# An AdaLN transformer block: row scores copied out of their PSUM banks before the softmax

## The chip, the cores and the metric

The kernel runs on one core of a Trainium2 chip. The time is the device time of one execution in microseconds (us). The profile is one execution taken by the hardware profiler. The engines in it are PE (TensorE matmuls), PEld (TensorE weight loads), DVE (VectorE), ACT (ScalarE), POOL (GpSimd) and SP (SyncE, which issues nearly all DMA here). Each engine works through its own queue in order; an instruction that waits holds up all that stand behind it on that engine.

## The reference

`x` is (8, 1024, 512), viewed as eight sequences; a modulation vector from `cond` gives shift, scale and gate. The block is

```python
mod = silu(condition) @ Wada + bada          # six parts
xm  = layernorm(x) * (1 + sc_a) + sh_a
q, k, v = split(xm @ Wqkv)                   # 16 heads of 32
attn = softmax(where(causal, q k^T * scale, -inf))
x = x + gt_a * ((attn @ v) @ Wproj + bproj)
xm = layernorm(x) * (1 + sc_m) + sh_m
x = x + gt_m * (gelu(xm @ W1 + b1) @ W2 + b2)
```

All of it is float32.

## The kernel before

**Tiling.** The 8 x 1024 tokens are cut into 16 blocks `n` of 512 tokens, two for each sequence. Heads are taken in four groups `g` of four heads. The large products (q, k, v, up, down) are done by a Strassen scheme, so each of them is seven smaller products whose results are combined by ACT and DVE as they leave the three single PSUM banks `bank`. All products of this kind are issued from one helper (line 217) and are called the linear work below.

**Two kinds of attention.** Odd blocks, and the first two, compute the scores twice: once for the row maxima (`sc`, line 1613) and once transposed (`st`, line 1721), with the exponential on ACT (line 1734). The second half of a sequence attends to 1,024 keys, so it is always done that way. The even blocks from n = 2 on (seven of them: 2, 4, ... 14) are done "by rows", in `attend_rows` and `rows_unit` (line 1998). Their stretch of the time is called a row stage. A row stage has ten units. A unit is one query tile of 128 rows against 512 keys, or two query tiles whose widths add to 512 (384 + 128, or 256 + 256), for four heads.

**One row unit.** PE writes its scores `rows_sc` into four PSUM banks at once (line 2021). These four banks are one tile with the tag `st` and one buffer; the score units and the transposed scores of the other blocks use the same tile. DVE adds the causal mask in place (line 2028), takes the row maximum of each query tile (line 2032) and turns it into a bias (line 2034). ACT makes the exponentials from PSUM into an SBUF page `rows_p`, one instruction for each head and query tile, each followed by the reading of its sum (line 2040). When the last exponential is done, PE may write the next scores. After that DVE transposes the page in 32 x 32 blocks (line 2053), SP sends it to an image in DRAM (line 2068, `scatter`), and when an image of a head group is whole, SP fetches it back as `turned` pages (line 2143) and PE multiplies them with v (line 2155). There are three pages (`p0` to `p2`), shared by the raw pages of row units (at most two between issue and scatter, counted in `raws`) and by the fetched pages.

**What sets the order.** The program is written out once by a planner in the kernel's own Python: it keeps a planned clock for each engine (`now`), adds a planned duration for each instruction (`note`, `note_act`, `note_dma`), and remembers when a tile is planned to be written (`written`) or free (`left`). Linear work is a set of generators; before a score or row unit, `step_aside` (line 1471) goes on with linear work while the unit would have to wait longer for its tile than the linear work. `until` (line 1467) does linear work until a condition holds. DVE work that can be put off stands in `row_jobs` and `jobs` and is issued by `run_row_jobs` (line 560) and `run_jobs` when DVE is planned to be at most 2 us ahead of PE; row jobs come first. So planned durations decide the order of all instructions on all queues, that of the DMA issues on SP too; on the chip the order is fixed and semaphores make each instruction wait for its data.

The weights for the linear work go through a ring of eight SBUF buffers filled by SP (lines 358 to 362).

Of the kernel before, what the change touches and what calls it, by code (L numbers as in the profile page):

```python
# [22 lines left out]
def kernel(  # L23
# [44 lines left out]
    HPG = P // hd  # L68
# [13 lines left out]
    small = ctx.enter_context(tc.tile_pool(name="small", bufs=2))  # L82
# [12 lines left out]
    written, left = {}, {}  # L95
# [17 lines left out]
    def note(engine, ns, reads=(), writes=(), port=False):  # L113
        start = max(now[engine], due(reads, writes))
        if port:
            start = max([start] + [b for a, b in pool_spans if a <= start < b])
        end = start + ns
        now[engine] = end
        if engine == "POOL":
            pool_spans.append((start, end))  # L120
            del pool_spans[:-16]
        for k in reads:
            left[k] = max(left.get(k, 0.0), end + SYNC)
        for k in writes:
            written[k] = end + SYNC
        return end
# [19 lines left out]
    def note_act(ns, func, reads=(), writes=()):  # L146
        if func is not None and table[0] != func:
            table[0] = func
            ns += TABLE
        note("ACT", ns, reads, writes)  # L150
# [1267 lines left out]
    def start(it):  # L1418
        thread = [it, None]
        sides.append(thread)  # L1420
        advance(thread)
# [127 lines left out]
    def diagonals(parts, sc):  # L1549

        if parts[-1][4] == parts[0][4]:
            first, span = parts[0][3] - P, len(parts) * P
            return span, sc[:, :, first : first + span].rearrange("p j (a c) -> p j a c", c=P)
        return 2 * P, sc.rearrange("p j (a c) -> p j a c", c=2 * P)[:, :, :, P:]
# [443 lines left out]
    def rows_unit(n, g, parts):  # L1998

        until(lambda: n in projected)  # L2000
        until(lambda: free_p and len(raws) < 2)
        slot = take_slot()
        raws.append(slot)
        reads = [("qT", n), ("kT", n)]
        step_aside(reads, ["st", ("p", slot)])
        name = f"{n}_{g}_{parts[0][0]}"
        sc = ps_st.tile([P, HPG, TB], F32, tag="st", name=f"rows_sc_{name}")
        raw = pp.tile([P, HPG * TB], F32, tag=f"p{slot}", name=f"rows_p_{name}")
        mx, minus = (
            small.tile([P, 2, HPG], F32, tag=f"rows_{kind}", name=f"rows_{kind}_{name}")  # L2010
            for kind in ("max", "minus")
        )
        for gg in {part[4]: None for part in parts}:
            if (n, gg) not in totals_of:
                totals_of[n, gg] = small.tile(
                    [P, HPG, NTT], F32, tag=f"rows_sum_{gg}", name=f"rows_sum_{n}_{gg}", bufs=1
                )
        for qt, kh, c0, w, gg in parts:
            for j in range(HPG):
                r = slice(j * hd, (j + 1) * hd)  # L2020
                nc.tensor.matmul(  # L2021
                    sc[:, j, c0 : c0 + w], qTs[n][r, gg, ts(qt, P)], kTs[n][r, gg, :w],
                    start=True, stop=True, skip_group_check=True,
                )
            note_pe(2 * COLUMN * w, "rows", reads, ["st"])
        span, place = diagonals(parts, sc)
        shape_of = mask.unsqueeze(1).unsqueeze(1)
        nc.vector.tensor_tensor(place, place, shape_of.to_broadcast(place.shape), ALU.add)
        note("DVE", 165 + 4.16 * span, ["st"])
        n_parts = len(parts)  # L2030
        for i, (qt, kh, c0, w, gg) in enumerate(parts):
            nc.vector.tensor_reduce(mx[:, i, :], sc[:, :, c0 : c0 + w], axis=AX.X, op=ALU.max)
            note("DVE", 170 + 4.14 * w, ["st"], [("mxr", slot)])
        nc.vector.tensor_scalar(minus[:, :n_parts], mx[:, :n_parts], -scale, None, ALU.mult)  # L2034
        note("DVE", 120, [], [("mxr", slot)], port=True)
        places, at = [], 0
        for i, (qt, kh, c0, w, gg) in enumerate(parts):
            tile_of = raw[:, at : at + HPG * w].rearrange("p (b k j x) -> p j k b x", b=NTT, j=HPG, x=hd)
            for j in range(HPG):
                nc.scalar.activation(  # L2040
                    tile_of[:, j], sc[:, j, c0 : c0 + w].rearrange("p (k b x) -> p k b x", b=NTT, x=hd),
                    AF.Exp, bias=minus[:, i, j : j + 1], scale=scale, accum_out=totals_of[n, gg][:, j, qt : qt + 1],
                )
                note_act(480 + 0.82 * w, "exp", ["st", ("mxr", slot)], [("p", slot)])
            places.append((qt, w, gg, at))
            at += HPG * w
            in_sums[n, gg] += 1
            if in_sums[n, gg] == NTT:
                written["sums", n, gg] = written["p", slot]
                start(inverses(n, gg))  # L2050

        def turned():
            nc.vector.transpose(raw, raw)  # L2053
            note("DVE", 2320, [("p", slot)], [("p", slot)])
            start(scatter())

        def scatter():
            yield [("p", slot)], []
            for qt, w, gg, at in places:
                count = w // P  # L2060
                if (n, gg) not in images:
                    images[n, gg] = [
                        kept.tile([P, 2, NTT, size, P], F32, tag=f"image_{gg}_{size}", name=f"image_{n}_{gg}_{size}")
                        for size in (2, 4)
                    ]
                for a in range(NTT):
                    into = images[n, gg][qt // 2][:, qt % 2, a, :count, :]
                    nc.sync.dma_start(
                        into.rearrange("(b k) s e -> k b (s e)", k=hd),
                        raw[ts(a, hd), at : at + HPG * w].rearrange("k (b f) -> k b f", b=NTT),  # L2070
                    )
                    note_dma(230 * count, [("p", slot)])
                in_image[n, gg] += count
            left["p", slot] = now["DMA"] + LAND
            raws.remove(slot)
            give_slot(slot)
            for gg in {part[4]: None for part in parts}:
                if in_image[n, gg] == 10:
                    written["image", n, gg] = now["DMA"] + LAND + LATE / 2
                    start(gather(n, gg))  # L2080

        row_jobs.append((turned, [("p", slot)]))

    def inverses(n, g):

# [202 lines left out]
```

## Time and profile before

| | |
|---|---|
| median of 3 runs | 3538.62 us (3537.95 to 3542.44) |
| the profiled execution | 3545.22 us |
| its span | 3543.5 us |
| PE busy | 3377.7 us (95%) |
| DVE busy | 2339.5 us (66%) |
| ACT busy | 1248.8 us (35%) |
| POOL busy | 1762.9 us (50%) |
| mean granted TensorE clock | 0.985 |

A row of a group reads: line, engine, operation, output <- inputs, shapes, count | busy time in us, mean ns of one | idle time of the engine just before them and what ended it. A row of waits reads: who waited <- for whom: total us, times, longest us. A row of the timeline reads: start, length in us, engine, line, operation; in square brackets the idle time before it and what ended it. A row of a stretch reads: from:to, its length, busy time (and count) of PE, PEld, DVE, ACT and POOL, then the mean granted clock, the share of time in which the DMA engines were busy, and GB/s.

### The profile page before, as it was taken

What the parts mean: (1) busy time and instruction counts of PE and PEld (TensorE: products, weight loads), DVE (VectorE), ACT (ScalarE), POOL (GpSimd) and SP (SyncE); (2) the same over time, 40 slices, a digit from 0 to 9 for tenths busy, and PEclk for the clock granted to TensorE, in tenths of its full rate; (3) what the DMA queues carried; (4) which work ended last, traced back from release to release, by engine and by line L of the source; (5) the groups of instructions that cost most, each with busy time, mean ns of one, the idle gap of its engine ahead of it and who ended that gap; (6) DMA issues with size and microseconds to landing.
All of it is one profiled execution on the core that took longest, in us unless ns stands there. A gap on an engine that the chain in (4) does not pass through costs nothing.

```text
span 3543.5 us, 118795 instructions
## 1 busy us (share of the span) xinstructions
PE 3377.7 (95%) x52861; PEld 1705.4 (48%) x52861; DVE 2339.5 (66%) x2562; ACT 1248.8 (35%) x1970; POOL 1762.9 (50%) x1710
## 2 busy tenths in 40 slices
PE   8999889999899998999999999999999999899999
PEld 4444445444454444544454454544555445454455
DVE  5766577657577575775767757676677667566563
ACT  2334333343233532335223353333523334232521
POOL 3667713756037650477405674066731667208640
PEclk9999999999999999999999999999999999999999
DMA  6843487537875378753886538865498555973344
GB/s 198 263 148 112 150 235 214 155 109 213 245 209 155 102 226 239 209 153 103 247 233 189 153 109 264 253 185 142 127 284 236 147 142 154 284 221 111 92 135 138
DMA packets 502579, 645.42 MB, mean 182 GB/s; under 512 B 40365, under 2 KB 334061, under 8 KB 498485
## 3 DMA queue, kind: packets, MB, share of 16 engines
q1 hardware_dynamic: 501952, 637.80, 60.8%
q8 instruction: 416, 6.82, 0.8%
q14 instruction: 95, 0.77, 0.1%
q10 hardware_dynamic: 116, 0.03, 0.0%
HBM read 506.31 MB, written 129.27 MB: 179 GB/s over the span
## 4 chain that ended last, share of the span: by engine, by line
PE 37%; DMA 6%; POOL 4%; DVE 3%; issue 1%; SPq 1%; ACT 1%; DVEq 0%; POOLq 0%; ACTq 0%
PE bank L217 27%; PE sc L1613 3%; POOL pT L1856 3%; PE po L1762 2%; PE st L1721 2%; DMA held_m<-xm_m 1%; DMA turned<-image 1%; PE rows_sc L2021 1%; PE st L1709 1%; PE po L2155 1%; DVE mx L1628 1%; DMA w<-in_L_cond_Wproj_dram 1%; DMA hat_m<-held_m 1%; PE bank L1783 0%; DMA w<-in_L_cond_W_dram 0%
## 5 line engine op out<-in xcount | busy, mean ns | idle before, releaser
L1856 POOL TENSOR_TENSOR pT<-pT,pT 128x512 f32<-128x512 f32 (+3 forms) x918 | 981.9, 1104 | 250.5 <-ACT pT L1734 197.2
L217 PE MATMUL bank<-w,hT 128*32 128x256 f32 x14336 | 822.4, 380 | 0.9 <-ACT y_d L204 0.9
L1734 ACT ACTIVATE pT<-st 128x2048 f32<-128x2048 f32 x218 | 409.5, 1879 | 762.1 <-PE st L1721 573.9
L217 PEld LDWEIGHTS bank<-w,hT 128*32 128x32 f32 x14336 | 457.0, 110 | 372.7 <-issue 87.5
L1628 DVE TENSOR_REDUCE mx<-sc 128x4 f32<-128x2048 f32 (+3 forms) x271 | 499.4, 1859 | 183.0 <-PE sc L1613 179.7
L217 PE MATMUL bank<-xm_m,w 128*32 128x256 f32 x8192 | 506.6, 384 | 28.8 <-DMA w<-in_L_cond_W_dram 19.7
L2040 ACT ACTIVATE rows_p<-rows_sc,rows_minus 128x256 f32<-128x256 f32 (+3 forms) x448 | 229.6, 534 | 448.0 <-DVE rows_minus L2034 246.4
L217 PE MATMUL bank<-t_m,w 128*32 128x256 f32 x6144 | 382.9, 380 | 1.1 <-DVE hT L208 0.9
L217 PEld LDWEIGHTS bank<-xm_m,w 128*32 128x32 f32 x8192 | 257.8, 111 | 245.5 <-issue 66.4
L217 PEld LDWEIGHTS bank<-t_m,w 128*32 128x32 f32 x6144 | 190.7, 110 | 179.8 <-issue 58.3
L217 PE MATMUL bank<-xm_a,w 128*32 128x256 f32 x3968 | 252.1, 392 | 26.0 <-DVE xm_a L782 16.3
L217 PE MATMUL bank<-w,qT 128*32 128x512 f32 x2048 | 242.0, 610 | 16.3 <-DMA w<-in_L_cond_Wproj_dram 16.2
L1613 PE MATMUL sc<-kT,qT 32*128 32x512 f32 (+3 forms) x2168 | 250.6, 546 | 6.9 <-DVE mx L1628 3.5
L1762 PE MATMUL po<-pT,v 128*32 128x512 f32 (+3 forms) x2176 | 232.0, 515 | 4.5 <-POOL pT L1739 4.4
L1721 PE MATMUL st<-qT,kT 32*128 32x512 f32 (+3 forms) x2176 | 228.5, 508 | 0.0
L208 DVE TENSOR_TENSOR hT<-bank,u_u 128x512 f32<-128x512 f32 x181 | 121.4, 683 | 113.0 <-PE bank L217 110.6
L217 PEld LDWEIGHTS bank<-xm_a,w 128*32 128x32 f32 x3968 | 131.7, 113 | 131.3 <-issue 29.2
L217 PE MATMUL bank<-t_a,w 128*32 128x256 f32 x2944 | 184.4, 383 | 2.6 <-DVE qT L208 2.1
L2053 DVE STREAM_TRANSPOSE rows_p<-rows_p 128x2048 f32<-128x2048 f32 x70 | 160.9, 2298 | 36.2 <-ACT rows_p L2040 35.5
L1625 DVE TENSOR_TENSOR sc<-sc,mask 128x1024 f32<-128x1024 f32 (+1 forms) x89 | 90.5, 1017 | 124.4 <-PE sc L1613 91.9
L1129 ACT ACTIVATE hT<-hT,cols 128x512 f32<-128x512 f32 x256 | 164.4, 711 | 22.8 <-DVE hT L208 21.6
L655 POOL TENSOR_SCALAR rstd_a<-mv_a 128x4 f32<-128x4 f32 x14 | 3.2, 231 | 333.6 <-DVE mv_a L634 333.1
(268 smaller groups left out, 4152.9 us busy)
## 6 DMA issues: line engine op xcount, KB each, us to landing
w<-in_L_cond_W_dram SPq DMA_DIRECT2D x384, 256.0 KB
w<-kept_up_S SPq DMA_DIRECT2D x256, 256.0 KB
w<-kept_down_S SPq DMA_DIRECT2D x256, 256.0 KB
w<-kept_qkv_S SPq DMA_DIRECT2D x180, 256.0 KB
w<-in_L_cond_Wqkv_dram SPq DMA_DIRECT2D x147, 256.0 KB
image<-rows_p SPq DMA_DIRECT2D x112, 256.0 KB
turned<-image SPq DMA_DIRECT2D x28, 1024.0 KB
turned<-image SPq DMA_DIRECT2D x56, 512.0 KB
```

Of the source, the lines that this page charges most:

```text
L208: nc.vector.tensor_tensor(out, src, other, op)
L217: nc.tensor.matmul(ps[r, :], columns, rhs, start=start, stop=stop, skip_group_check=True)
L1129: nc.scalar.activation(hT[:, i, :], hT[:, i, :], AF.Gelu, bias=cols[:, O_B1 + f : O_B1 + f + 1])
L1613: nc.tensor.matmul(sc[:, j, c0 : c0 + w], qTs[n][r, gg, ts(qt, P)], keys_of(n, kh)[r, gg, :w], start=True, stop=True, skip_group_check=True,)
L1625: nc.vector.tensor_tensor(place, place, shape_of.to_broadcast(place.shape), ALU.add)
L1628: nc.vector.tensor_reduce(maxima[n, gg][:, kh, qt, :], sc[:, :, c0 : c0 + w], axis=AX.X, op=ALU.max)
L1721: nc.tensor.matmul(st[:, j, c0 : c0 + w], kT[r, gg, ts(k % NTT, P)], qT[r, gg, TB - w :], start=False, stop=True, skip_group_check=True,)
L1734: nc.scalar.activation(pT[:, :, :used], st[:, :, :used], AF.Exp, scale=scale)
L1762: nc.tensor.matmul(po[r, TB - w :], v[:, k % NTT, g * P + j * hd : g * P + (j + 1) * hd], pT[:, j, c0 : c0 + w], start=(k == 0), stop=last ...
L1856: nc.gpsimd.tensor_tensor(into, into, pT[:, j, c0 : c0 + w], ALU.add)
L2040: nc.scalar.activation(tile_of[:, j], sc[:, j, c0 : c0 + w].rearrange("p (k b x) -> p k b x", b=NTT, x=hd), AF.Exp, bias=minus[:, i, j : j ...
L2053: nc.vector.transpose(raw, raw)
```

## The change

The scores of a row unit leave their banks at once. For each query tile of the unit, DVE adds the mask to the last 128 columns (the diagonal block) on the way from PSUM into the page, and ACT copies every other block of 128 columns. Maxima, exponentials and sums are then made in the page, in place: `largest` is a row job that takes the maxima on DVE, `exponentials` a thread that starts when they are planned to be there, and the transpose is a row job behind it. The planner also counts 2 us more before the scatter of a page is issued. `bufs=2` writes out what the pool `small` has anyway.

```diff
-        span, place = diagonals(parts, sc)
-        shape_of = mask.unsqueeze(1).unsqueeze(1)
-        nc.vector.tensor_tensor(place, place, shape_of.to_broadcast(place.shape), ALU.add)
-        note("DVE", 165 + 4.16 * span, ["st"])
-        n_parts = len(parts)
-        for i, (qt, kh, c0, w, gg) in enumerate(parts):
-            nc.vector.tensor_reduce(mx[:, i, :], sc[:, :, c0 : c0 + w], axis=AX.X, op=ALU.max)
-            note("DVE", 170 + 4.14 * w, ["st"], [("mxr", slot)])
-        nc.vector.tensor_scalar(minus[:, :n_parts], mx[:, :n_parts], -scale, None, ALU.mult)
-        note("DVE", 120, [], [("mxr", slot)], port=True)
         places, at = [], 0
-        for i, (qt, kh, c0, w, gg) in enumerate(parts):
+        shape_of = mask.rearrange("p (b x) -> p b x", x=hd).unsqueeze(1)
+        for qt, kh, c0, w, gg in parts:
             tile_of = raw[:, at : at + HPG * w].rearrange("p (b k j x) -> p j k b x", b=NTT, j=HPG, x=hd)
-            for j in range(HPG):
-                nc.scalar.activation(
-                    tile_of[:, j], sc[:, j, c0 : c0 + w].rearrange("p (k b x) -> p k b x", b=NTT, x=hd),
-                    AF.Exp, bias=minus[:, i, j : j + 1], scale=scale, accum_out=totals_of[n, gg][:, j, qt : qt + 1],
+            into = tile_of[:, :, w // P - 1]
+            some = sc[:, :, c0 + w - P : c0 + w].rearrange("p j (b x) -> p j b x", x=hd)
+            nc.vector.tensor_tensor(into, some, shape_of.to_broadcast(into.shape), ALU.add)
+            note("DVE", 165 + 4.16 * P, ["st"], [("raw", slot)])
+            for k in range(w // P - 1):
+                nc.scalar.copy(
+                    tile_of[:, :, k],
+                    sc[:, :, c0 + k * P : c0 + (k + 1) * P].rearrange("p j (b x) -> p j b x", x=hd),
                 )
-                note_act(480 + 0.82 * w, "exp", ["st", ("mxr", slot)], [("p", slot)])
+                note_act(585, None, ["st"], [("raw", slot)])
             places.append((qt, w, gg, at))
             at += HPG * w
...
+        def largest():
+            for i, (qt, w, gg, at) in enumerate(places):
+                some = raw[:, at : at + HPG * w].rearrange("p (a j x) -> p j a x", j=HPG, x=hd)
+                nc.vector.tensor_reduce(mx[:, i, :], some, axis=AX.XY, op=ALU.max)
+                note("DVE", 170 + 4.14 * w, [("raw", slot)], [("mxr", slot)])
+            n_parts = len(places)
+            nc.vector.tensor_scalar(minus[:, :n_parts], mx[:, :n_parts], -scale, None, ALU.mult)
+            note("DVE", 120, [], [("mxr", slot)], port=True)
+            start(exponentials())
+
+        def exponentials():
+            yield [("mxr", slot)], []
+            for i, (qt, w, gg, at) in enumerate(places):
+                some = raw[:, at : at + HPG * w].rearrange("p (a j x) -> p j a x", j=HPG, x=hd)
+                for j in range(HPG):
+                    nc.scalar.activation(
+                        some[:, j], some[:, j], AF.Exp, bias=minus[:, i, j : j + 1], scale=scale,
+                        accum_out=totals_of[n, gg][:, j, qt : qt + 1],
+                    )
+                    note_act(480 + 0.82 * w, "exp", [("mxr", slot)], [("p", slot)])
...
+            row_jobs.append((turned, [("p", slot)]))
 
         def turned():
             nc.vector.transpose(raw, raw)
             note("DVE", 2320, [("p", slot)], [("p", slot)])
+            written["p", slot] += 2000
             start(scatter())
...
-        row_jobs.append((turned, [("p", slot)]))
+        row_jobs.append((largest, [("raw", slot)]))
```

More of the change, by code (lines that the diff above doesn't have):

```diff
@@ L2009, in rows_unit @@
         mx, minus = (
-            small.tile([P, 2, HPG], F32, tag=f"rows_{kind}", name=f"rows_{kind}_{name}")
+            small.tile([P, 2, HPG], F32, tag=f"rows_{kind}", name=f"rows_{kind}_{name}", bufs=2)
             for kind in ("max", "minus")
@@ L2043, in rows_unit @@
                 )
-                note_act(480 + 0.82 * w, "exp", ["st", ("mxr", slot)], [("p", slot)])
+                note_act(585, None, ["st"], [("raw", slot)])
             places.append((qt, w, gg, at))
             at += HPG * w
[L2047 to L2050, printed above, removed]
+        def largest():
[7 more added lines that the diff above has]
+            start(exponentials())
@@ new lines, in exponentials @@
+        def exponentials():
[8 more added lines that the diff above has]
+                    note_act(480 + 0.82 * w, "exp", [("mxr", slot)], [("p", slot)])
+                in_sums[n, gg] += 1
+                if in_sums[n, gg] == NTT:
+                    written["sums", n, gg] = written["p", slot]
+                    start(inverses(n, gg))
+            row_jobs.append((turned, [("p", slot)]))
```

## The prediction

> **What bounds the kernel now.** I read the head of the page first, then the stretches of the seven row stages against those between them, then PE's waits, and then the timeline of the first row stage.
>
> ```profile
> span 3543.5 us, 118795 instructions
> PE 3377.7 (95%) x52861; PEld 1705.4 (48%) x52861; DVE 2339.5 (66%) x2562; ACT 1248.8 (35%) x1970; POOL 1762.9 (50%) x1710
> ```
>
> PE is the bound: it is busy for all but 165.8 us (3543.5 - 3377.7). The change gives PE neither more nor less to do, so all it can win is a part of that idle time, and of what a slowed clock costs behind it.
>
> ```profile
> 416.40:544.20 127.80, 103.77 (x1440) 49.34 (x1440) 94.90 (x104) 45.75 (x134) 17.46 (x20) 0.91 0.78 227
> ...
> 818.00:989.70 171.70, 155.55 (x2508) 83.33 (x2504) 120.27 (x135) 50.79 (x142) 45.77 (x39) 0.97 0.82 236
> ...
> sum 1194.80, PE 1087.34 PEld 582.47 DVE 833.04 ACT 365.18 POOL 314.58; mean PE 155.33 PEld 83.21 DVE 119.01 ACT 52.17 POOL 44.94
> ```
>
> These are the row stages, the first (n = 2), the second, and the sum of all seven. PE is idle there for 107.5 us (1194.80 - 1087.34), 24.0 us of it in the first stage alone, where the granted clock is 0.91. DMA engines are busy for about 0.8 of the time.
>
> ```profile
> sum 1536.50, PE 1513.92 PEld 730.19 DVE 1014.04 ACT 617.50 POOL 1005.51; mean PE 252.32 PEld 121.70 DVE 169.01 ACT 102.92 POOL 167.58
> ```
>
> In the six stretches between them PE is idle for only 22.6 us. So the idle time that can be fought for lies in the row stages, and the question is how much of it is owed to the four score banks.
>
> ```profile
> PE bank L217 <- DMA w<-in_L_cond_W_dram: 19.7, 3, 7.5
> PE po L2155 <- DMA turned<-image: 17.1, 19, 3.2
> PE bank L217 <- DVE xm_a L782: 16.3, 2, 8.6
> PE bank L217 <- DMA w<-in_L_cond_Wproj_dram: 16.2, 11, 4.5
> PE rows_sc L2021 <- ACT rows_p L2040: 12.5, 4, 7.9
> ...
> PE bank L217 <- ACT p_k L197: 4.4, 3, 2.4
> ...
> PE bank L217 <- ACT xm_m L788: 2.8, 2, 2.1
> ...
> PE sc L1613 <- ACT rows_p L2040: 2.1, 2, 1.4
> ```
>
> Little of it: waits that end with the last exponential of a row unit add to 14.6 us (12.5 + 2.1, six waits). The larger ones end with weights, with fetched pages, or with modulated rows (`xm_a`, itself behind a DMA, below). The planner has put linear work beside the rest of the time in which the banks are held.
>
> ```profile
> 425.51 1.71 PE L2021 MATMUL rows_sc<-kT,qT 32*128 32x512 f32 x8 [2.60 <-ACT rows_p L2040]
> ...
> 435.34 1.15 PE L2021 MATMUL rows_sc<-kT,qT 32*128 32x384 f32 x16 [1.09 <-ACT rows_p L2040]
> 444.36 2.09 PE L2021 MATMUL rows_sc<-kT,qT 32*128 32x512 f32 x8 [7.87 <-ACT rows_p L2040]
> 446.38 7.91 PE L217 MATMUL bank<-w,qT 128*32 128x512 f32 x56
> 455.23 1.03 PE L2021 MATMUL rows_sc<-kT,qT 32*128 32x384 f32 x11 [0.94 <-ACT rows_p L2040]
> ...
> 446.58 2.54 DVE L1802 RECIPROCAL top_rec<-top_rec 128x128 f32<-128x128 f32 x3
> ...
> 449.29 1.28 POOL L1830 TENSOR_TENSOR qT<-top_rec 128x512 f32<-128x512 f32 x1 [26.49 <-DVE top_rec L1802]
> ```
>
> All four waits of line 2021 lie in the first row stage, 2.60 + 1.09 + 7.87 + 0.94 = 12.5 us. Units start 9.0 to 10.9 us apart there, each at the moment the banks come free: in this place the hold of the banks is the pace. Behind the longest wait stands the output projection (446.38). It could have started on its first three head groups; for the fourth it needs the quotient that POOL makes at 449.29, late because DVE came to the reciprocals only at 446.58.
>
> **The change, part by part.**
>
> ```profile
> L2028 DVE TENSOR_TENSOR rows_sc<-rows_sc,mask 128x1024 f32<-128x1024 f32 x42 | 51.3, 1221 | 27.6 <-PE rows_sc L2021 27.3
> L2028 DVE TENSOR_TENSOR rows_sc<-rows_sc,mask 128x512 f32<-128x512 f32 x28 | 19.3, 691 | 10.6 <-PE rows_sc L2021 10.5
> L2032 DVE TENSOR_REDUCE rows_max<-rows_sc 128x4 f32<-128x2048 f32 x28 | 64.2, 2292 | 1.0
> L2040 ACT ACTIVATE rows_p<-rows_sc,rows_minus 128x512 f32<-128x512 f32 x112 | 75.5, 686 | 163.6 <-DVE rows_minus L2034 48.2 <-DMA turned<-image 34.6 <-issue 27.5
> L2053 DVE STREAM_TRANSPOSE rows_p<-rows_p 128x2048 f32<-128x2048 f32 x70 | 160.9, 2298 | 36.2 <-ACT rows_p L2040 35.5
> L197 ACT COPY hT<-bank 128x512 f32<-128x512 f32 x41 | 23.9, 582 | 96.4 <-PE bank L217 96.3
> ```
>
> *Mask add.* A stage's ten units hold 16 query tiles, so 70 adds become 7 x 16 = 112 of 128x512, at 691 ns each 77.4 us in place of 70.6 (51.3 + 19.3). The 6.8 us more are spread over row stages in which DVE is idle for 361.8 us (1194.80 - 833.04); cost 0, and 1 us per stage if DVE were full.
>
> *Copies.* A tile of width w has w/128 - 1 of them: per stage 4 x 3 + 4 x 2 + 4 x 1 = 24, in all 168, at 582 ns 97.8 us more on ACT, 14.0 us per stage. ACT is busy for 45.75 of 127.80 us in the first stage and 52.17 in the mean one, so it would stand at 47% and 39%; cost 0. Without that cover it would be 14 us per stage.
>
> *Maxima, exponentials, transposes* keep number and size. Their sources move to SBUF, and no row here shows a row maximum of that form; I take the PSUM rows (2292 and 686 ns). The nearest SBUF row of that size is the transpose, 2298 ns, so the two ends agree. [...]
>
> *The hold of the banks.* After the last matmul it was mask, maxima and all exponentials, 7.8 to 9.7 us (the 9.0 to 10.9 us above less some 1.2 us of matmuls, the 1.15 us row). It becomes one or two adds (0.7 to 1.4 us) beside at most three copies (1.7 us), plus what stands ahead of them on ACT. That takes away the 14.6 us of waits. What is late next: the 7.87 us wait has the projection behind it, which then waits for the quotient. I take half of it, between 0 (the quotient comes as late as now) and 7.87 (DVE, rid of a block of mask and maxima ahead of the reciprocals, brings it sooner). Term a: 14.6 - 3.9 = 10.7 us won, ends 6.7 and 14.6.
>
> ```profile
> 425.50:436.00 10.50, 8.11 (x80) 3.44 (x84) 8.79 (x9) 3.71 (x10) 0.00 (x0) 0.67 0.64 178
> 436.00:450.60 14.60, 6.73 (x44) 1.67 (x36) 12.20 (x11) 3.76 (x16) 1.28 (x1) 0.65 0.68 192
> ```
>
> *The clock.* In these two stretches around the waits the granted clock is 0.67 and 0.65. If it is one half or one, it was one half for 6.9 and 10.2 us, 17.1 us in all, 10.3 of which PE may have been idle. Half of the other 6.8 us is lost: term b between 0 and 3.4 us, I take 2.0 since some idle stays.
>
> ```profile
> ACT rows_p L2040 <- DVE rows_minus L2034: 246.4, 29, 13.7
> ```
>
> *Queue order on ACT.* ACT stood at the head of a unit's exponentials for 246.4 us, with bank copies queued behind; now the exponentials are issued when the maxima are planned to be there. The new wait, of the copies for PE's scores, is at most the 1.2 us of matmuls, with bank copies behind it. `largest` on DVE may wait for ACT's copies, 1.7 us, with bank combines behind it; it is issued when they are planned to be done, so 0 if ACT keeps to plan. PE's waits on ACT's bank work, 4.4 and 2.8 us above, bound this: term c between 0 and 7.2, I take 2.0, as only part of them lies in row stages.
>
> ```profile
> 416.46 1.15 PE L2021 MATMUL rows_sc<-kT,qT 32*128 32x256 f32 x16
> ...
> 427.90 3.76 SPq L2068 DMA_DIRECT2D image<-rows_p  x8
> ```
>
> *The longer chain.* From scores to the first image issue a unit with little in its way takes 11.4 us now. The adds are 0.2 us longer (2 x 691 against 1221 ns) and there are two hand-overs more, so 0.2 to 0.9 us on the chip. The planner puts the scatter 2 us later on SP's queue, and with it the fetch and the products. The 19 waits for fetched pages (17.1 us) get longer by at most 19 x 0.9 = 17 us, or vanish as their places move back (-17). Nearest is the 0.2 us that rows give: term d, 19 x 0.2 = 4 us lost.
>
> *The order of everything else* moves as well, since planned times change; I give it no sign. `bufs=2` costs nothing, as two buffers were there.
>
> Sum: -10.7 - 2.0 - 2.0 + 4 = -10.7 us. The profiled execution took 3545.2 us (its span and 1.7 us), 6.6 us over the median; from it the sum gives 3534.5, and from the median of the runs 3528 us, which I forecast (0.3% less).
>
> **The rivals.**
>
> *The idle time only changes its name* (no change). The projection waits for the quotient as long as it waited for the banks, so term a is 6.7, b is 1, c is 0, d stays: -3.7 us, 3535 us. For it speaks POOL's 26.49 us wait; against it, that DVE's queue gets shorter just there.
>
> *The banks do not come free sooner.* The copies stand in ACT's queue behind another unit's exponentials (four of 512 columns at 686 ns, 2.7 us, or eight smaller ones), and an add behind a maximum and a transpose. Then a and b are near 0 and d remains: 3543 us. Against it speaks that ACT is idle over half the time.
>
> *SP's queue is upset* (slower). Image writes go out in the same queue as weights and rows of the normalised input.
>
> ```profile
> SPq L2068 <- DVE rows_p L2053: 29.9, 13, 7.1
> ```
>
> ```profile
> 883.67 5.01 SPq L2068 DMA_DIRECT2D image<-rows_p  x8
> 888.72 1.89 SPq L728 DMA_DIRECT2D hat_a<-held_a  x4
> ```
>
> ```profile
> 897.04 1.01 DVE L782 TENSOR_SCALAR xm_a<-hat_a,gaina,shifta 128x512 f32<-128x512 f32 x2 [4.11 <-DMA hat_a<-held_a]
> ```
>
> In the second row stage one unit's eight image issues take SP 5.0 us; the loads of `hat_a` stand behind them, DVE waits for these, and PE's longest wait for `xm_a` (8.6 us, above) ends here. Planned chains change in every row stage, so one scatter more can come to stand ahead of such a load, or of the first weights of a step. If it does in each of the six later stages at 5.0 us, that is 30 us: 3528 + 30 = 3558 us. It decides from 10.7 / 6 = 1.8 us per stage on. For it: the waits that bound those stages are of this kind already, and a scatter now hangs on two more hand-overs while SP waits in order. Against it: the planner's 2 us hold it back until its page is turned, which should shrink the 29.9 us, and a load may as well come to stand ahead of a scatter.
>
> **How the numbers follow.** No change from noise can be told within about 0.2%, 7.1 us (3531.5 to 3545.7). Chances: forecast 0.43; idle time renamed 0.16 and banks not freed 0.08, both within the 0.2%; SP's queue 0.33. So faster 0.43, same 0.24, slower 0.33. The forecast's own range is 3513 (all of a, b and c: 14.6 + 3.4 + 7.2 = 25.2 won, nothing lost on d) to 3531.5. Below 3512 the vanishing of d would have to be added, 1 in 20; above 3557 lies about the upper half of the last rival, less than 3 in 20. The range is 3512 to 3557.
>
> **What the profile of the changed kernel would show.** Waits of line 2021 and 1613 for a row unit's exponentials are gone; PE's idle time in the first row stage falls from 24.0 to some 14 us and its clock rises from 0.91. 168 copies of 128x512 stand on ACT at about 582 ns, 112 adds on DVE at about 691; the maxima keep 2292 ns at 2,048 elements. ACT's 246.4 us behind the bias shrink. The projection of the first stage starts before 446 us. The forecast is wrong if the first stage's idle time stays at 24 us with the quotient or a page as its releaser (first two rivals), or if waits of line 217 for weights and `xm_a` in the six later stages (83.5 us of idle time together, 107.5 - 24.0) grow by 1.8 us a stage or more (last rival). Row stages as a whole tell it: 107.5 us of idle PE before.

## The result, and the profile after

The changed kernel takes 3602.58 us (3596.89 to 3608.24), the kernel before 3539.32 us on the same chip: a ratio of 1.0177, 95% interval 1.0160 to 1.0195. It is slower by 63 us; the forecast was 3528 us, and the range ended at 3557 us. The profiled execution took 3596.89 us.

The head of the page:

```profile
span 3595.1 us, 118983 instructions
...
PE 3378.0 (94%) x52861; PEld 1714.1 (48%) x52861; DVE 2315.1 (64%) x2554; ACT 1392.0 (39%) x2194; POOL 1761.7 (49%) x1713
```

PE does the same work (3377.7 us before). Its idle time went from 165.8 to 217.1 us, 51.3 us more, and the span grew by 51.6. So the whole loss in this execution is PE waiting, and the question is for whom.

The stretches of the seven row stages, from the first to the last score matmul of each (the first stage, and the sum), and below them the sum of the six stretches between:

```profile
414.00:528.00 114.00, 93.19 (x1302) 44.63 (x1301) 88.12 (x97) 58.26 (x155) 18.85 (x21) 0.94 0.76 221
...
sum 1126.00, PE 1005.60 PEld 538.72 DVE 765.76 ACT 442.26 POOL 299.86; mean PE 143.66 PEld 76.96 DVE 109.39 ACT 63.18 POOL 42.84
```

```profile
sum 1641.00, PE 1583.95 PEld 776.58 DVE 1038.91 ACT 674.83 POOL 1010.29; mean PE 263.99 PEld 129.43 DVE 173.15 ACT 112.47 POOL 168.38
```

The row stages are shorter than before (1126 us against 1194.80) and hold 120.4 us of idle PE (107.5 before). The stretches between are longer (1641 against 1536.50) and hold 57.1 us (22.6 before). Two thirds of the new idle time, 34.5 us, lie in the stretches between the row stages, where the prediction had not looked for any.

PE's waits after the change:

```profile
PE po L2173 <- DMA turned<-image: 37.8, 23, 7.6
PE bank L217 <- ACT xm_m L788: 16.7, 3, 6.8
...
PE bank L217 <- POOL qT L1830: 8.5, 1, 8.5
PE bank L217 <- DVE p_v L194: 8.0, 3, 4.9
PE bank L217 <- DMA w<-in_L_cond_W_dram: 7.3, 2, 6.2
PE bank L217 <- DVE xm_a L782: 7.0, 2, 4.6
PE bank L217 <- ACT p_v L197: 6.7, 4, 3.5
...
PE sc L1613 <- DVE rows_p L2032: 6.2, 7, 0.9
...
PE sc L1613 <- ACT rows_p L2035: 5.3, 6, 1.0
...
PE rows_sc L2021 <- DVE rows_p L2032: 3.9, 2, 3.2
```

No wait of the score matmuls for a row unit's exponentials is left. In its place the banks are waited for until an add or a copy has read them: 3.9 + 6.2 + 5.3 = 15.4 us (a fourth wait, of 0.2 us, is not shown), against 14.6 before. The wait for fetched pages has more than doubled (17.1 to 37.8), and waits for rows (`xm_m`) and combines (`p_v`) of ACT and DVE have come up.

*Adds and copies take turns.* The groups of the new instructions in the changed kernel (busy us, mean ns | idle time before them, and what ended it):

```profile
L2035 ACT COPY rows_p<-rows_sc 128x512 f32<-128x512 f32 x168 | 90.0, 589 | 319.6 <-DVE rows_p L2032 256.5 <-DMA image<-rows_p 31.4 <-DMA w<-kept_qkv_S 13.6
...
L2032 DVE TENSOR_TENSOR rows_p<-rows_sc,mask 128x512 f32<-128x512 f32 x112 | 76.4, 682 | 111.3 <-PE rows_sc L2021 45.7 <-ACT rows_p L2035 45.5 <-DMA image<-rows_p 12.1
```

and one unit on its timeline:

```profile
1266.23 1.15 PE L2021 MATMUL rows_sc<-kT,qT 32*128 32x384 f32 x16
...
1266.30 2.28 DVE L2046 TENSOR_REDUCE rows_max<-rows_p 128x4 f32<-128x2048 f32 x1
...
1268.61 2.37 DVE L2049 TENSOR_SCALAR rows_minus<-rows_max 128x4 f32<-128x4 f32 x1
...
1270.89 0.68 DVE L2032 TENSOR_TENSOR rows_p<-rows_sc,mask 128x512 f32<-128x512 f32 x1
...
1271.60 1.07 ACT L2035 COPY rows_p<-rows_sc 128x512 f32<-128x512 f32 x2 [9.20 <-DVE rows_p L2032]
...
1272.71 0.69 DVE L2032 TENSOR_TENSOR rows_p<-rows_sc,mask 128x512 f32<-128x512 f32 x1 [1.14 <-ACT rows_p L2035]
```

The scores stand at 1267.4. The two copies need 1.07 us and ACT is free, but they start at 1271.60, when DVE has made the first add, which stood behind another unit's maximum and bias; and the second add waits 1.14 us for the two copies. So the banks come free at 1273.4, six microseconds after the scores. Some 2.2 us of them are a bias that took 2.37 us, where the median of the 70 is 0.17 us; what held it is not shown. The prediction had copies and adds side by side. In the trace they take turns: none of the 168 copies overlaps any of the 112 adds, ACT waits 256.5 us for adds, most of it for what stands ahead of them on DVE, and DVE's adds wait 45.5 us for copies. What makes one wait for the other the trace does not show. A unit's scores lie across four banks with a head in each, so every add and every copy touches all four.

Adds and copies also write the same page, so the page could be what orders them, or the banks. The run `act_copies_all` (below), in which ACT makes all copies and DVE adds the mask afterwards in the page, helps to tell the two apart. Its first unit has two tiles of 256 columns:

```profile
418.05 2.06 ACT L2034 COPY rows_p<-rows_sc 128x512 f32<-128x512 f32 x4 [0.56 <-PE rows_sc L2021]
```

```profile
419.23 2.50 DVE L2044 TENSOR_TENSOR rows_p<-rows_p,mask 128x512 f32<-128x512 f32 x2 [3.31 <-ACT rows_p L2034]
```

The add into the first tile starts at 419.23, while ACT copies the second tile into the same page until 420.11. In that run 15 adds overlap copies of their own unit in this way; in the changed kernel the second add of a unit, which goes to columns of its own too, began only after the last copy of the first tile had ended, in all 42 units with two tiles. So the page is not what orders the second add, and of the two the banks are what is left. For the first add and the copies of the same tile, whose blocks lie interleaved in the page, no run tells page from banks.

*The way from the scores to the transposed page* got longer: from a unit's first score matmul to the end of its last transpose it takes 14.5 us before and 19.1 us after (mean of 70 units), and for the last unit of a stage 15.2 and 25.0 us. The last unit of the third row stage shows how (DVE, then SP, then PE):

```profile
1423.95 0.69 DVE L2032 TENSOR_TENSOR rows_p<-rows_sc,mask 128x512 f32<-128x512 f32 x1 [1.14 <-ACT rows_p L2035]
...
1435.26 2.34 DVE L2046 TENSOR_REDUCE rows_max<-rows_p 128x4 f32<-128x1536 f32 x2
...
1445.92 2.30 DVE L2070 STREAM_TRANSPOSE rows_p<-rows_p 128x2048 f32<-128x2048 f32 x1
```

```profile
1442.91 9.11 SPq L358 DMA_DIRECT2D w<-in_L_cond_W_dram  x4
...
1452.79 5.28 SPq L2086 DMA_DIRECT2D image<-rows_p  x8
...
1480.24 0.54 SPq L2161 DMA_DIRECT2D turned<-image  x1
```

```profile
1487.76 1.08 PE L2173 MATMUL po<-turned,v 128*32 128x256 f32 x8 [7.57 <-DMA turned<-image]
```

The page is filled at 1424.6, but its maxima are a job of their own now and start at 1435.26, behind the maxima of the next block's score units. The page is turned at 1448.2, its image goes out behind 9.11 us of weights, the last of what is fetched back is issued at 1480.24, and at 1487.76 PE has stood 7.57 us for a fetched page.

### The profile page after: what moved, and what is told of

Read it like the earlier page. It is cut to its first block, busy times and chain, and to the rows that moved or that the text cites. A ratio compares the mean times of both kernels' runs of the same rounds, so it can differ in the third digit from the quotient of the medians.

```text
span 3595.1 us, 118983 instructions
## 1 busy us (share of the span) xinstructions
PE 3378.0 (94%) x52861; PEld 1714.1 (48%) x52861; DVE 2315.1 (64%) x2554; ACT 1392.0 (39%) x2194; POOL 1761.7 (49%) x1713
## 5 line engine op out<-in xcount | busy, mean ns | idle before, releaser
L217 PE MATMUL bank<-xm_m,w 128*32 128x256 f32 x8192 | 507.8, 384 | 31.8 <-ACT xm_m L788 16.7
L2058 ACT ACTIVATE rows_p<-rows_p,rows_minus 128x256 f32<-128x256 f32 (+3 forms) x448 | 245.3, 550 | 67.2 <-DVE rows_minus L2049 67.0
L2035 ACT COPY rows_p<-rows_sc 128x512 f32<-128x512 f32 x168 | 90.0, 589 | 319.6 <-DVE rows_p L2032 256.5
L2046 DVE TENSOR_REDUCE rows_max<-rows_p 128x4 f32<-128x1024 f32 (+3 forms) x112 | 161.3, 1471 | 13.8 <-ACT rows_p L2035 13.7
L1739 POOL TENSOR_SCALAR_AFFINE_SELECT pT<-pT 128x512 f32<-128x512 f32 x144 | 103.2, 734 | 133.9 <-ACT pT L1734 133.8
```

Source lines behind the costliest of these rows:

```text
L217: nc.tensor.matmul(ps[r, :], columns, rhs, start=start, stop=stop, skip_group_check=True)
L1739: nc.gpsimd.affine_select(diagonal, diagonal, pattern=[[0, HPG], [1, P]], compare_op=ALU.is_ge, fill=0.0, base=0, channel_multiplier=-1,)
L2046: nc.vector.tensor_reduce(mx[:, i, :], some, axis=AX.XY, op=ALU.max)
L2058: nc.scalar.activation(some[:, j], some[:, j], AF.Exp, bias=minus[:, i, j : j + 1], scale=scale, accum_out=totals_of[n, gg][:, j, qt : qt ...
```

## The experiments

Two questions: does the loss come from the path of the data (copies, turns, longer chain), or from the order that the planner writes when it is told other durations? And which of the things that it is told? All ratios are to the kernel before on the same chip, with their 95% interval; the times are medians.

**The bank's hold as the planner had it before.** The data take the new path, but the planner is told that the four banks stay taken as long as with the exponentials in them. First for all units:

```diff
+        left["st"] += 2400 + sum(HPG * (480 + 0.82 * part[3]) for part in parts)
```

> The changed kernel, but the planner is told that the score banks stay taken until the old end (maxima and exponentials later), while on the chip they come free early. Theory 'order' (row units are pulled ahead of linear work because the banks are planned to be free sooner, and that order costs the time): back to 3535 to 3550 us. Theory 'chain' (a unit's way from scores to image has grown from 14.5 us to 19.1 us until its page is transposed, by two more passes through the queues of DVE and ACT, so fetched pages come late): it stays at 3585 us or above, since that way stays as long.

Measured: 3552.61 us, 1.0029 [1.0013, 1.0045], 3 us over the range of 'order' and far under that of 'chain'. Some 53 of the 63 us are gone, with every copy and add still there. But the way from scores to page did not stay as long: it fell to 17.1 us in the mean and 21.0 for the last unit of a stage, and PE's waits for fetched pages to 20.9 us. So this run alone does not part the two theories; the planner told of the turns, below, does so better. Then for the first six units of a stage alone, and (with the condition turned round) for the last four alone:

```diff
+        if not in_last[0]:
+            left["st"] += 2400 + sum(HPG * (480 + 0.82 * part[3]) for part in parts)
```

> The changed kernel with the planner told the old, long hold of the banks, but only behind the first six units of a row stage (other row units follow them). If the loss comes from these six being set closer to one another, this gets back most of what hold_told got back: about 3560 us. If it comes from the last four, between which the next block's score units stand, about 3595 us. If any other order would have lost as much (the plan of the kernel before being a lucky one), somewhere between with no system.

> The same, but the old hold is told only behind the last four units of a row stage. Score units of the next block then stand further from row units, and the maxima and the transpose of a row unit get on DVE ahead of them: if that is the cause, about 3560 us and the way to the transposed page of the last unit falls from 25.0 us to 20 us or less; if the first six units are the cause, about 3595 us.

Measured: 3573.68 us, 1.0086 [1.0056, 1.0116], and 3574.39 us, 1.0081 [1.0052, 1.0109]. Each of them gets back about half of the loss (32 and 34 us of 63), which is neither the 3560 nor the 3595 us that a single place would have given. As one order can lie 20 us from another for no reason that is known (below), these two runs do not show more; with `hold_last` the last unit still takes 23.8 us from scores to page.

**Parts of the change undone.** The 2 us before the scatter left out; all four blocks copied by ACT, with the mask added afterwards in the page; maxima and exponentials issued at once behind the copies.

```diff
-            written["p", slot] += 2000
```

> The changed kernel without the 2 us that the planner adds before a scatter. If these 2 us delay images, the theory 'chain' gives 10 to 20 us back (3582 to 3592 us). If they keep SP from waiting in order for DVE, it gets slower by 5 to 15 us. Theory 'order' gives no direction, within 10 us of 3602.

Measured: 3587.15 us, 1.0118 [1.0091, 1.0146]. By the ratios that is 21 us less than the changed kernel, where 'chain' had 10 to 20, but no less than that kernel reaches when it is nudged, that is, when its planner is told a time that is 0.15 us off (below), so this run says nothing of the 2 us.

```diff
-            nc.vector.tensor_tensor(into, some, shape_of.to_broadcast(into.shape), ALU.add)
-            note("DVE", 165 + 4.16 * P, ["st"], [("raw", slot)])
-            for k in range(w // P - 1):
+            for k in range(w // P):
...
         def largest():
+            for into in diagonal_of:
+                nc.vector.tensor_tensor(into, into, shape_of.to_broadcast(into.shape), ALU.add)
+                note("DVE", 700, [("raw", slot)], [("raw", slot)], port=True)
```

> All four 128-column blocks of a tile are copied by ACT and the mask is added by DVE in the page, ahead of the maxima, so copies and adds no longer take turns at the banks. If that taking of turns (ACT's copies waited 256.5 us for DVE's adds) is what costs, 3565 to 3580 us and ACT's wait for the add is gone; by 'order' and by the rest of 'chain' it stays within 10 us of 3602.

Measured: 3576.44 us, 1.0094 [1.0073, 1.0116]. Nothing takes turns at the banks here, and 29 us are back, as forecast for the case that the turns cost, though ACT makes 280 copies in place of 168. It lies under all three orders of the changed kernel that were timed, by 6 us under the best of them, which the intervals do not tell apart.

```diff
-        row_jobs.append((largest, [("raw", slot)]))
+        largest()
+        exponentials()
+        row_jobs.append((turned, [("p", slot)]))
```

> The copying alone: maxima and exponentials are issued right behind the copies, as in the kernel before, not as jobs, and without the 2 us. Banks are still freed early, in the plan and on the chip. Theory 'chain': way to the transposed page back to about 16 us, 3540 to 3560 us. Theory 'order': 3585 us or above.

Measured: 3671.72 us, 1.0376 [1.0347, 1.0405]. It is 70 us slower still, and its mean from scores to page, 19.3 us, is no shorter, where 'chain' had 16. So undoing the postponing wins nothing back; as the order moved with it, what of the 70 us is owed to what is not shown.

**The order alone.** The kernel before, unchanged but for one number that the planner is told, when the banks come free: 2.5 us too early (shown), 2.5 us too late, 0.15 us too late and 0.15 us too early.

```diff
                 start(inverses(n, gg))
+        left["st"] -= 2500
```

> The kernel before, with the one difference that its planner believes the banks to be free 2.5 us before the last exponential is planned to end; on the chip nothing is freed earlier. If the order that follows from an early release is bad by itself, or the old order is a lucky one that any shift spoils, 3560 to 3590 us. If the order is robust and only the new data path costs, within 8 us of 3540.

> The kernel before with its planner told that the banks come free 2.5 us later than planned so far; the chip as it was. Theory 'plan too early' (what costs is a plan that counts on the banks before the chip gives them): a plan on the late side costs little, 3535 to 3552 us. Theory 'lucky order' (the old plan's constants fit one order, and any other order loses 20 to 60 us): 3560 us or above, as with 2.5 us too early (3594).

> The kernel before with the banks planned to be free 0.15 us later: no belief that matters changes, but the instruction order does from the first row stage on. 'Plan too early': within 8 us of 3540. 'Lucky order': 3555 us or above.

> The same, 0.15 us earlier. 'Plan too early': within 8 us of 3540. 'Lucky order': 3555 us or above.

Measured: 3594.21 us, 1.0140 [1.0115, 1.0165]; 3567.57 us, 1.0074 [1.0058, 1.0090]; 3547.89 us, 1.0014 [1.0004, 1.0024]; 3570.09 us, 1.0079 [1.0057, 1.0101]. A planner that believes the banks free 2.5 us too early costs 50 us without any copy. Its waits of PE:

```profile
PE rows_sc L2021 <- ACT rows_p L2040: 32.4, 14, 7.9
PE po L2156 <- DMA turned<-image: 29.8, 19, 7.8
PE sc L1613 <- ACT rows_p L2040: 15.1, 18, 3.0
```

47.5 us behind exponentials (14.6 before) and 29.8 behind fetched pages (17.1): the scores are written ahead of linear work that could have gone first. But 0.15 us in either direction costs 5 (late) and 28 us (early), and 2.5 us too late costs 25. 'Lucky order' forecast a loss of this kind for all four, and three have it (the first is 4 us over its range); 'plan too early' got the 5 us, but neither the 25 nor the 28. The order of the kernel before is the best of the five, and two orders that differ by next to nothing can lie nearly half of the 63 us apart.

**The path alone.** The new path of the data at the old places: adds, copies, maxima and exponentials issued where mask, maxima and exponentials were, with the old notes to the planner, so that PE, SP and POOL have the order of the kernel before, instruction for instruction. Then the same with each copy made twice, one behind the other.

```diff
-        nc.vector.tensor_tensor(place, place, shape_of.to_broadcast(place.shape), ALU.add)
+        for qt, kh, c0, w, gg in parts:
...
+            nc.vector.tensor_tensor(into, some, blocks_mask.to_broadcast(into.shape), ALU.add)
+            for k in range(w // P - 1):
+                nc.scalar.copy(
...
         note("DVE", 165 + 4.16 * span, ["st"])
```

> The new data path alone: adds and copies into the page, maxima and exponentials in place, but all written where the old ones stood and planned with the old durations, so that PE, SP and POOL have exactly the order of the kernel before, and ACT and DVE too but for the new instructions. Theory 'order': 3535 to 3550 us. Theory 'data path': 3580 us or above; between them, the share above 3542 is the data path's.

> As same_plan, with each of ACT's copies made twice (168 copies of 0.59 us more, 98 us of ACT). 'Order': within 10 us of same_plan, since ACT has room. If ACT's copies are what costs, the distance of same_plan to 3542 doubles.

Measured: 3588.10 us, 1.0128 [1.0107, 1.0148], and 3647.14 us, 1.0293 [1.0271, 1.0314]. This is the cleanest reading of the path: 45 us at an unchanged order, as 'data path' had it, and 59 us more for another 98 us of copies (168 x 0.59; they add 85.2 us to ACT's busy time, as a copy starts before the one ahead of it ends). In the first, the waits of DVE for copies, and the waits of PE that grew:

```profile
DVE rows_max L2046 <- ACT rows_p L2038: 46.8, 28, 2.8
...
DVE rows_p L2036 <- ACT rows_p L2038: 41.5, 42, 1.4
```

```profile
PE bank L217 <- DVE p_v L194: 18.9, 6, 4.5
...
PE bank L217 <- DVE hT L208: 8.7, 8, 1.9
PE bank L217 <- DVE u_k L208: 7.4, 1, 7.4
PE bank L217 <- DVE u_u L208: 7.3, 8, 1.7
...
PE bank L217 <- DVE p_u L194: 7.0, 5, 2.5
```

The same waits of PE in the kernel before:

```profile
PE bank L217 <- DVE p_u L194: 1.5, 2, 1.0
...
PE bank L217 <- DVE u_u L208: 1.4, 3, 0.5
...
PE bank L217 <- DVE u_k L208: 1.3, 1, 1.3
...
PE bank L217 <- DVE hT L208: 0.9, 2, 0.5
...
PE bank L217 <- DVE p_v L194: 0.7, 1, 0.7
```

Five rows, 5.8 us before and 49.3 us now: 43.5 us. PE's idle time grew by 41.1 us in all (3588.4 us of span less 3381.5 of busy PE, against 165.8); what other rows gained and lost nearly cancels. With the copies doubled DVE waits 165.6 us for them (88.3 with one), and PE 34.2 us for `p_v` alone:

```profile
DVE rows_max L2046 <- ACT rows_p L2038: 88.0, 28, 4.3
DVE rows_p L2036 <- ACT rows_p L2038: 77.6, 42, 2.4
```

```profile
PE bank L217 <- DVE p_v L194: 34.2, 6, 8.5
```

Not all of the second step is waiting: of 57.9 us more span, 36.2 are idle time of PE, and 21.7 are busy time (3403.2 against 3381.5 us for the same matmuls), at a granted clock of 0.976 against 0.985.

One of the six `p_v` waits, with one copy each, shows the way from ACT to PE:

```profile
1755.35 0.65 DVE L2036 TENSOR_TENSOR rows_p<-rows_sc,mask 128x512 f32<-128x512 f32 x1
...
1756.04 1.07 ACT L2038 COPY rows_p<-rows_sc 128x512 f32<-128x512 f32 x2 [4.52 <-DVE rows_p L2036]
...
1757.14 0.69 DVE L2036 TENSOR_TENSOR rows_p<-rows_sc,mask 128x512 f32<-128x512 f32 x1 [1.14 <-ACT rows_p L2038]
...
1757.75 2.33 DVE L2046 TENSOR_REDUCE rows_max<-rows_p 128x4 f32<-128x1536 f32 x2
...
1761.02 0.69 DVE L194 COPY p_v<-bank 128x512 f32<-128x512 f32 x1
...
1761.76 1.51 PE L217 MATMUL bank<-w,xm_a 128*32 128x256 f32 x12 [4.54 <-DVE p_v L194]
```

ACT is idle before the copies, and none of PE's rows above names them. But DVE stands 1.14 us for them with the maxima behind, and behind the maxima stands the combine that frees a linear bank; PE waits for that one 4.54 us. The other waits of these rows were not followed one by one; that they grow with the number of copies speaks for the same way.

**The planner told of the turns.** The changed kernel, with a copy planned to start only when the add before it is done, and the add of the second query tile only when the copies are. Then the same with the banks told free 2.5 us later, 0.15 us later and 0.15 us earlier; and, to compare, the changed kernel itself with the banks told free 0.15 us later and earlier.

```diff
+        turns_of = []
...
-            note("DVE", 165 + 4.16 * P, ["st"], [("raw", slot)])
+            note("DVE", 165 + 4.16 * P, ["st", *turns_of], [("raw", slot)])
...
-                note_act(585, None, ["st"], [("raw", slot)])
+                note_act(585, None, ["st", ("raw", slot)], [("raw", slot)])
+                turns_of = [("raw", slot)]
```

> The changed kernel with the planner told the truth on one point: ACT's copies and DVE's adds of a unit take turns, so they are planned one behind the other (the planned hold grows by 0.7 to 1.9 us). If the loss comes from a plan that is wrong by that, 3570 us or less; if from the early release as such, or from the longer way, within 10 us of 3602.

> The changed kernel with its turns at the banks planned (3557) and the banks planned to be free 2.5 us later still, which is nearer to what the chip does when an add stands behind other work on DVE. 'Plan too early': 3540 to 3552 us. 'Lucky order': anything between 3550 and 3600.

> The changed kernel with the banks planned to be free 0.15 us later. 'Order': it moves by 5 to 50 us either way, most likely down, as 3602 lies at the upper end of what the nudged kernels gave (3548 to 3594). 'Data path': within 8 us of 3602.

> The same, 0.15 us earlier: 'order' 5 to 50 us away from 3602, 'data path' within 8 us.

> Planner told that copies and adds take turns, and in addition that the score banks come free 0.15 us later than that. If the 45 us between the changed kernel (3602.6 us) and the version told of the turns (3557.3 us) are owed to what the planner is told, this stays well under the changed kernel and its two nudged versions (3585.2 and 3594.8 us): 3550 to 3580 us. If the 3557 us were a lucky order, a nudge throws it back among them: 3583 to 3603 us.

> The same with the banks told free 0.15 us earlier. If what the planner is told decides: 3550 to 3580 us. If the order's scatter decides: 3583 to 3603 us.

| kernel | told 0.15 us early | as it is | told 0.15 us late | mean |
|---|---|---|---|---|
| before | 1.0079 | 1 | 1.0014 | 1.0031 |
| changed, told of the turns | 1.0066 [1.0045, 1.0086] | 1.0045 [1.0030, 1.0060] | 1.0076 [1.0058, 1.0094] | 1.0062 |
| changed | 1.0141 [1.0116, 1.0166] | 1.0177 [1.0160, 1.0195] | 1.0112 [1.0085, 1.0139] | 1.0143 |

In us these are 3565.65, 3557.26 and 3566.45 for the told ones, 3594.77, 3602.58 and 3585.21 for the changed one. None of these three told orders is as slow as any of the three changed ones, which luck alone would do once in twenty times; the means differ by 0.8%, 29 us. So telling the planner of the turns is probably worth something, as forecast (3550 to 3580 us for both nudges). It is not shown beyond doubt: the intervals of the slowest told and the fastest changed order overlap, and told 2.5 us more, which is a told order too, it took 3586.60 us, 1.0122 [1.0088, 1.0155], inside the changed family. So later is not better in itself, and why the long hold of the first experiment did so well (1.0029) is not settled: it may be an order that happened to be good. In the nudged changed kernels the order moved the time by 13 and 23 us, as 'order' had it.

In the told kernel PE's waits for fetched pages (32.7 us), for `xm_m` (15.7) and for the quotient (8.6) are still there; what went is the score matmuls' waits for adds and copies (15.4 to 3.1 us) and most of those for `p_v` (8.0 + 6.7 to 1.1). The way from scores to page is longer than in the changed kernel, 20.9 us in the mean and 26.7 for the last unit of a stage (19.1 and 25.0 there), and the kernel is 45 us faster. So the longer way by itself is not what costs the time. No kernel of this study beats the one before.

## Why the prediction was wrong, point by point

*PE's work.* Right: 3377.7 and 3378.0 us; in the profiled execution all of the loss is waiting.

*Durations.* Right: 168 copies at 589 ns (582 taken), 112 adds with a median of 691 ns, maxima of 2,048 elements at 2266 ns (2292 taken). For the sources in SBUF the groups of the changed kernel show:

```profile
L2058 ACT ACTIVATE rows_p<-rows_p,rows_minus 128x512 f32<-128x512 f32 x112 | 79.5, 714 | 12.2 <-DVE rows_minus L2049 12.1
...
L2046 DVE TENSOR_REDUCE rows_max<-rows_p 128x4 f32<-128x2048 f32 x28 | 63.5, 2266 | 13.8 <-ACT rows_p L2035 13.7
...
L2058 ACT ACTIVATE rows_p<-rows_p,rows_minus 128x128 f32<-128x128 f32 x112 | 43.2, 387 | 0.0
```

An exponential of 512 columns takes 714 ns (686 before), one of 128 columns 387 (389): +28 and -2 ns, and the maximum is 26 ns shorter. The prediction took the PSUM rows for them. Beside a loss of 63 us these differences are small: for the 112 exponentials of 512 columns, 112 x 28 ns = 3.1 us of ACT.

*Copies, "cost 0", and `largest` "0 if ACT keeps to plan".* This is the step that failed first. The cover was looked up as a share (ACT at 47% and 39%), but these copies, in the middle of a chain between two engines, were not covered by the idle time of one of them. At an unchanged order the new path, copies and turns, costs 45 us, and once more the copies 59 us: 0.60 us of the kernel for each us of copies (59 / 98). `largest`, put at 0, waits 13.7 us for copies in the changed kernel (the second row above), on top of the 45.5 us of the adds. The bound that the prediction named for "without that cover", 14 us a stage, is 98 us in all; the two runs lie about half way. In the changed kernel itself the order is another, so how much of its 63 us is this step is argued, not measured.

*Term a, the hold of the banks (-10.7).* Failed: 14.6 us of waits became 15.4 us with other names, since the hold is one or two adds and up to three copies in turn, plus what stands ahead of them on two queues. The 7.87 us wait of the first stage turned into 8.5 us for the quotient from POOL: the first rival's mechanism, at its full size where half was taken. The projection goes on at 446.55, not before 446 us. That stage's idle time fell from 24.0 to 20.8 us (114.00 - 93.19), not to 14, and its clock rose from 0.91 to 0.94, as forecast.

*Term b, the clock (-2).* Failed with it: the mean granted clock is 0.982 (0.985 before).

*Term c, ACT freed of the head-of-queue wait (-2).* Failed: 246.4 us behind the bias became 256.5 us behind the adds, where 1.2 us of matmuls was to be the most that a copy waits for. PE's waits on ACT's bank work, 4.4 and 2.8 us before and the bound of the term, are 16.7 us for `xm_m` and 6.7 for `p_v` now.

*Term d, the longer chain (+4).* Right sign, wrong size: it took the two hand-overs (0.2 to 0.9 us, the upper end an estimate that no row gives; between the last copy of a first tile and the second add a hand-over took 0.03 to 0.04 us, in all 42 units with two tiles) and not that the maxima become a job that stands behind others on DVE. The chain grew by 4.6 us in the mean and 9.8 us for the last unit; the waits for fetched pages grew by 20.7 us (4 taken, 17 as the bound). That such a growth must cost as much in the end does not follow: the told kernel has the longer chain, 32.7 us of these waits, and 45 us less.

*"The order of everything else: no sign."* It has one. The order before is better than its neighbours, and the new one is worse than its own. From the means of the table, with three orders each: 29 us between the changed and the told family, 11 us between the told family and that of the kernel before, 12 us by which the changed kernel lies above the mean of its family ((1.0177 - 1.0143) x 3540), and 11 us by which the kernel before lies below that of its own. They add to 63 us, since each step starts where the one before it ends. The second is within the scatter of either family, so whether the new path costs anything under a planner that knows it isn't settled; and the last two, 23 us, are put down to the luck of two single orders.

*The rivals.* "SP's queue is upset" named the right side and the wrong mechanism: waits for `xm_a` and for the first weights fell (16.3 to 12.8 us, 5.8 of them now for ACT's part, and 19.7 to 7.3 us). Its price, 3558 us, lies over the end of the range, and its upper half is a chance of 0.165, a little more than the "less than 3 in 20" that was left above it. "The banks do not come free sooner" named what happened to the banks, but stopped at 3543 us, since it priced only what would not be won.

## What to carry to other kernels

Work that is split over two engines that read the same PSUM banks may still be one chain: in this kernel ACT and DVE took turns in every unit (no overlap of 168 copies and 112 adds), copies stood 256.5 us for adds and adds 45.5 us for copies with other work queued behind them, and a low share of busy time on either engine (39% and 64%) was no cover. Where an order is planned from durations, a change must tell the planner which instructions take turns; else it plans banks free that are not. One plan that was 2.5 us early cost 50 us here, and PE stood 47.5 us behind exponentials in it. And a single order is one draw: nudge the planner by a tenth or two of a microsecond in both kernels before a difference of one per cent is put down to the change.

## What was unexpected of the hardware

- Reads of the same four banks by ACT and DVE never overlapped in the changed kernel (168 copies, 112 adds), while writes of both into different columns of one page did in `act_copies_all`. In the rows shown hand-overs took 0.03 to 0.04 us on top of the work (an add ending at 1756.00 and the copies starting at 1756.04, these ending at 1757.11 and the next add starting at 1757.14), so the hand-over itself is cheap here and the queueing is not: the copies stood 256.5 us for adds, most of it for what was ahead of these on DVE.
- A wait was passed on along the queues: at the unchanged order, 168 copies for which DVE waits 88.3 us go with 43.5 us more of PE's waits on five kinds of bank, though none of these waits ends with a copy.
- A planned time changed by 0.15 us moved a 3540 us program by 5 to 28 us when up or down from the kernel before, and by 13 to 23 us from the changed one, by the ratios of the table.
